# A list-scheduled Mamba layer and local transformer: a seventh tile for the broadcasts of B and C, paid with one tile for values and one for the shared sums, and a new order of all engines' work

## The chip, the core and the metric

The kernel runs on one core of a Trainium2 chip. The metric is the device time of one execution in microseconds (us); of several runs the median counts. A profiled execution gives a span, which is the time from the first to the last instruction, and its own device time.

The core's engines run side by side, each through its own list of instructions in order: PE (matrix products and transposes; results go to PSUM), DVE (vector work), ACT (activations and copies), POOL (elementwise work in SBUF), and SP, which here only issues DMAs. An instruction that waits for another engine or for a DMA holds everything behind it on its own engine.

## What is computed

The input x has 4096 rows of 256 numbers. Its layer-normed form xn goes into two branches, whose results are added to x:

```
x  = L0_attn_x
xn = _layernorm(x)
x  = x + mamba(xn) + ffn(xn)

# mamba, D_INNER 512, D_STATE 16
xz = xn @ in_proj_w.T;  x_inner, z = split(xz)
x_conv = silu(conv4(x_inner) + conv_b)
dt_lr, B, C = split(x_conv @ x_proj_w.T)          # 16 + 16 + 16 columns
dt = softplus(dt_lr @ dt_proj_w.T + dt_proj_b);   A = -exp(A_log)
h[t] = exp(dt[t] * A) * h[t-1] + (dt[t] * x_conv[t]) * B[t]
y[t] = sum over the 16 states of h[t] * C[t];     y += x_conv * D_param
out  = (y * silu(z)) @ out_proj_w.T

# ffn: two layers over the sequence of 4096 rows
q, k, v = shift(x) @ wqkv;  l2norm, scales, rotary;  8 heads, windows of 128 that see the one before
x = x + softmax(q k^T, masked) v @ wo
x = x + (a * gelu(g)) @ w2 + b2,   a, g = split(layernorm(shift(x)) @ w1 + b1)
```


## The kernel before, in words

**Work.** The transformer goes through 32 steps: layer 0 and then layer 1, each in 16 steps of 256 rows (two windows of 128). The Mamba branch goes through 8 blocks of 512 rows, each with 4 chunks of 128 channels, each chunk with 8 groups of two states: 256 groups in all. Block b and chunk c are tied to transformer step 4b + c, so one chunk of recurrences lies beside one transformer step.

**One group of the recurrence** (`recur`). Two DMAs bring rows of B and of C from memory, broadcast to all 128 partitions, into two tiles of the buffer `bc` (512 KB each). POOL multiplies the B tile by dt * x_conv in place (L793). For each of the two states ACT makes the decay (L802), DVE runs the recurrence over 512 steps (L807), ACT keeps the last state (L813), and DVE multiplies by the C tile (L817), writing over the B tile. In odd groups POOL adds the two states (L825); then PE sums the result into PSUM by transposes (L829). So the C tile is free after the second L817 and the B tile only after L829.

**Other parts that the change touches.** `normalize` loads rows of x into an `io` tile, and PE transposes them (L597). `project` makes q, k, v (L918), with L929 to L985 for norms and rotation and L945/L950 for the turned q and k; `attend` makes scores (L1017), mask and maximum (L1032), softmax (L1042), transposes (L1055), the copy to SBUF (L1059) and the product with v (L1071). `project_out` is L1112. `mlp` has means (L1141, after sums on POOL in L1149 and L1157), the up products (L1176), gelu (L1213), gains (L1221 on POOL), and the down products (L1247 in layer 0, L1266 in layer 1). `finish` (L546) adds a result to the shared sum of the two branches, which lies in an `io` tile, and stores it; `base_of` loads it again for the branch that comes second. `close` turns y back (L846 to L859), and `out_proj` is L879.

**The order.** Nothing is ordered by hand. Every operation is entered with an engine, a cost, a key (its step, less its own lead `soon`), and the tiles that it reads and writes. `Plan.order` is a list scheduler: it goes through time with these costs, gives each engine the open operation with the lowest key, and gives out the tiles of each buffer as they come free. Each engine's list is then issued as it came out, and on the chip the engines meet only at semaphores. On PE it takes into account that two kinds of product (`part="rows"`: L1017 and L734; `part="columns"`: L1071 and L702) use part of the array and that a change of kind costs. A DMA is counted as a fixed time plus its KB over a rate, and transfers on the way follow each other:

```
    TRANSFER, RATE = 2.2, 300.0
    ...
                w.end = moved = max(start + self.TRANSFER, moved) + w.late / self.RATE
```

Of the kernel before, what the change touches and what calls it, by code (L numbers as in the profile page):

```python
# [136 lines left out]
class Plan:  # L137
# [5 lines left out]
    TRANSFER, RATE = 2.2, 300.0  # L143
# [175 lines left out]
def mamba_and_local_transformer(  # L319
# [35 lines left out]
    rows_b = buffer("io", 3, [P, NW, D], any_first=True)  # L355
# [7 lines left out]
    values_b = buffer("v", 4, [P, INNER])  # L363
# [17 lines left out]
    spreads = buffer("bc", 6, [P, NG, TB])  # L381
# [73 lines left out]
    def load_small():  # L455
        dma(96, lambda: xpw.ap, lambda: xp_wT.rearrange("(c p) n -> p c n", p=P), writes=[xpw], soon=-0.25)
        for at_row in (0, DH):
            dma(32, lambda at_row=at_row: dtw.ap[at_row : at_row + DTR], lambda: dt_wT, writes=[(dtw, at_row)], soon=-1.44)
        dma(128, lambda: b2row.ap, lambda: b2_d[DEPTH - 1 : DEPTH, :].partition_broadcast(P), writes=[b2row], soon=-1.5)

    def load_qkv(l):
        for s in range(3):
            cut = slice(s * INNER, (s + 1) * INNER)
            dma(
                512, lambda cut=cut: wqkv.ap[:, :, cut],
                lambda cut=cut: wqkv_d[l][:, cut].rearrange("(k p) n -> p k n", p=P), writes=[(wqkv, s)], soon=0.31,
            )

    def load_rest(l):
        dma(512, lambda: wo.ap, lambda: wo_d[l].rearrange("(h p) n -> p h n", p=P), writes=[wo], soon=-0.19)  # L470
        for half in range(2):
            for m, n in ((0, WHOLE), (NM - 1, LAST)):
                to, of = w1_at(half, m), half * HID + m * MC
                dma(
                    n, lambda to=to, n=n: w1.ap[:, :, to : to + n],
                    lambda of=of, n=n: w1_d[l][:, of : of + n].rearrange("(k p) n -> p k n", p=P),
                    writes=[(w1, (half, m))], soon=-1.25,
                )
# [3 lines left out]
            lambda: w2_d[l][0:whole, :].rearrange("(m p) n -> p m n", p=MC), writes=[(w2, 0)], soon=0.22,  # L482
        )
        dma(42, lambda: w2.ap[0 : HID - whole, NM - 1, :], lambda: w2_d[l][whole:HID, :], writes=[(w2, 1)], soon=0.89)
# [28 lines left out]
        add("PE", 8.3, shift, [w1], [pb], soon=0.18)  # L513
        add("DVE", 0.4, bias, [pb], [b1, b1x], soon=0.05)
        add("DVE", 4.6, scale, [], [w1], port=True, soon=-0.44)
# [14 lines left out]
    def base_of(s):  # L530

        base = plan.value(rows_b)
        if s in sums:
            dma(256, lambda: base.ap, lambda: sums[s].ap, [sums[s]], [base], soon=-0.44)
            return base
        dma(256, lambda: base.ap, lambda: rows(x, s), writes=[base], soon=-1.19)
# [3 lines left out]
            ), [b2row], [base], soon=-0.45,  # L540
# [3 lines left out]
    def finish(s, po, base):  # L544

        add("DVE", 0.6, lambda: nc.vector.tensor_tensor(base.ap, halves(po), base.ap, ALU.add), [po], [base], soon=-0.18)  # L546
        if s in sums:
            dma(256, lambda: rows(out, s), lambda: base.ap, [base], soon=-1.5)
            return
        sums[s] = plan.fixed(dram.tile([P, NW, D], F32, tag=f"sum{s}", name=f"sum{s}"))  # L550
        dma(256, lambda: sums[s].ap, lambda: base.ap, [base], [sums[s]], soon=-1.32)
# [4 lines left out]
    def shift_column(l, s):  # L556
        now = xts[l, s]
        if s == 0:
            add("POOL", 0.14, lambda: nc.gpsimd.memset(now.ap[:, 1, 0:1], 0.0), [], [(now, 0)], soon=-0.18)
        else:  # L560
# [3 lines left out]
                [(old, 1)], [(now, 0)], soon=1.39,  # L564
            )

    def normalize(s):
# [5 lines left out]
        dma(256, lambda: xb.ap, lambda: rows(x, s), writes=[xb], soon=0.3)  # L573
# [27 lines left out]
        add("DVE", 1.1, stats, [xb], [mv], soon=1.36)  # L601
        add("ACT", 0.5, root, [mv], [rstd], soon=0.67)
        add("DVE", 0.6, centre, [mv, rstd], [xb], port=True, soon=-0.21)
        now = xts[0, s] = plan.value(tokens)
        add("PE", 0.44, turn, [xb], [pt], holds=[now], soon=1.2)
        add("ACT", 0.48, lambda: nc.scalar.copy(now.ap[:, :, 1:], halves(pt)), [pt], [(now, 1)], soon=0.88)
        shift_column(0, s)
        dma(256, lambda: xn_d[s].ap, lambda: now.ap[:, :, 1:], [(now, 1)], [xn_d[s]], soon=-0.42)
# [3 lines left out]
    def reload(s):  # L612
        now = xts[1, s] = plan.value(tokens)
        dma(256, lambda: now.ap[:, :, 1:], lambda: x1_d[s].ap, [x1_d[s]], [(now, 1)], soon=-0.52)
# [6 lines left out]
    def in_half(i):  # L621
# [3 lines left out]
            lambda: in_wT[:, i * DI : (i + 1) * DI].rearrange("(k p) n -> p k n", p=P), writes=[w], soon=-1.03,  # L625
# [3 lines left out]
    def in_proj(b, w, c, to):  # L629
# [9 lines left out]
        add("PE", 1.72, emit, [w, xms[b]], [pm], holds=[to], soon=-0.69)  # L639
        return pm  # L640

    def front_load(b):
        xm = xms[b] = plan.value(xms_b)
        for i in range(PB):
            s = b * PB + i
            dma(
                256, lambda i=i: xm.ap[:, :, i * TS : (i + 1) * TS], lambda s=s: xn_d[s].ap, [xn_d[s]], [(xm, i)], soon=-0.5
# [5 lines left out]
    def front_conv(b, c, w):  # L653
        xin, xc, tail = plan.value(rows_m), xcs[b], tails[b]
        edge = slice(c * (TAPS - 1), (c + 1) * (TAPS - 1))
        if b == 0:
            add("POOL", 0.14, lambda: nc.gpsimd.memset(xin.ap[:, 0 : TAPS - 1], 0.0), [], [(xin, 0)], soon=1.23)
        else:
# [3 lines left out]
                [(old, c)], [(xin, 0)], soon=1.08,  # L662
            )
        pm = in_proj(b, w, c, xin)
        add("ACT", 0.48, lambda: nc.scalar.copy(xin.ap[:, TAPS - 1 :], pm.ap), [pm], [(xin, 1)], soon=0.78)
        if b < NB - 1:
            add(
                "POOL", 0.14, lambda: nc.gpsimd.tensor_copy(tail.ap[:, edge], xin.ap[:, TB:]), [(xin, 1)], [(tail, c)], soon=0.17
# [5 lines left out]
            ), [], [pm], soon=-0.98,  # L674
# [8 lines left out]
        for j in range(TAPS - 1):  # L683
            add("DVE", 0.7, lambda j=j: tap(j), [xin, pm], [(xc, c) if j == TAPS - 2 else pm], soon=0.85)

    def silu(v):
# [4 lines left out]
        add("ACT", 4.52, emit, [], [v], soon=1.04)  # L691

    def front_dbl(b):
# [13 lines left out]
        add("PE", 1.75, emit, [xc, xpw], [px], holds=[xd, part], soon=-0.4, part="columns")  # L707
        add("ACT", 0.48, lambda: nc.scalar.copy(part.ap[0:n, 0:TB], px.ap[DH : DH + n]), [px], [part], alone=[px], soon=1.49)
# [5 lines left out]
        add("ACT", 0.48, lambda: nc.scalar.copy(xd.ap[DH : DH + DTR], xd.ap[0:DTR]), [(xd, 0)], [(xd, 1)], soon=-1.31)  # L714
        xds[b] = xd
        bc = bcs[b] = plan.fixed(dram.tile([2 * NS, TB], F32, tag=f"bc{b}", name=f"bc{b}"))
        dma(64, lambda: bc.ap, lambda: xd.ap[DTR:n, :], [(xd, 0)], [bc], soon=-0.54)

    def gate_conv(b, c, w):
# [4 lines left out]
        add("ACT", 0.48, lambda: nc.scalar.copy(sz.ap[:, c, :], pz.ap), [pz], [(sz, c)], soon=-1.26)  # L724

    def times(b, c):
# [12 lines left out]
        add("PE", 1.15, emit, [xd, dtw], banks2, holds=dts2, soon=0.95, part="rows")  # L739
        for i in range(2):  # L740
# [3 lines left out]
                ), [banks2[i]], [dts2[i]], soon=0.12,  # L744
# [3 lines left out]
    def prepare(b, c):  # L748

        if c % 2 == 0:  # L750
# [7 lines left out]
        add("ACT", 0.6, lambda: nc.scalar.activation(e.ap[:, n], dt.ap, AF.Abs), [dt], [e], soon=0.03)  # L758
        add("ACT", 0.6, lambda: nc.scalar.activation(dt.ap, dt.ap, AF.Relu), [], [dt], soon=-1.13)
        add("ACT", 0.54, lambda: nc.scalar.activation(e.ap[:, n], e.ap[:, n], AF.Exp, scale=-1.0), [], [e], soon=1.45)  # L760
        add(
            "DVE", 0.36, lambda: nc.vector.tensor_scalar(r.ap[:, n], e.ap[:, n], 1.0, -1.0, ALU.add, ALU.add),
            [e], [r], port=True, soon=1.5,
        )
        add("POOL", 1.22, lambda: nc.gpsimd.tensor_tensor(r.ap[:, n], e.ap[:, n], r.ap[:, n], ALU.subtract), [e], [r], soon=-0.4)
        add("ACT", 0.6, lambda: nc.scalar.activation(e.ap[:, n], e.ap[:, n], AF.Ln, bias=one_t), [], [e], soon=-0.27)
        add("POOL", 1.22, lambda: nc.gpsimd.tensor_tensor(dt.ap, dt.ap, r.ap[:, n], ALU.add), [r], [dt], soon=-1.2)
        add("POOL", 1.22, lambda: nc.gpsimd.tensor_tensor(dt.ap, dt.ap, e.ap[:, n], ALU.add), [e], [dt], soon=0.09)
# [653 lines left out]
```

## Time and profile before

| what | value |
|---|---|
| median of 3 runs | 1901.68 us (1895.44 to 1901.69) |
| the profiled execution's own time | 1896.31 us |
| its span | 1894.5 us |
| PE busy | 1853.1 us, 98% of the span |
| DVE, ACT, POOL busy | 1672.3 us (88%), 1588.8 us (84%), 1509.2 us (80%) |
| DMA | 334.69 MB, mean 177 GB/s |
| mean granted clock of PE | 0.993 |

How to read it: a row of the groups gives line, engine, operation, the tile written and the tiles read, shapes and count, then the busy time and the mean of one in ns, and last how long the engine stood idle before these instructions and who ended that. A row of the waits gives the sum, the number and the longest of such idle times. "SPq" is SP's queue of DMAs to issue: a wait there is the time in which the next DMA in order could not be issued. The float32 products of the program appear twice in the profile's counts.

### The profile page before, as it was taken

Reading aid. Unit: us, or ns where it says so; the run is one execution under the profiler, and the core shown is the slowest. Engines: PE = TensorE matmul, PEld = TensorE weight load, DVE = VectorE, ACT = ScalarE, POOL = GpSimd, SP = SyncE. Lnnn points to the kernel's source line nnn. Section 1 sums busy time; section 2 is a strip of 40 time slices with the busy share of each in tenths; the row PEclk is TensorE's granted clock in tenths of the full one; section 3 lists DMA queues with packets and bytes.
Section 4 is the critical chain, followed back from the end, with each engine's and each line's share of the span. In section 5 each row is a group of like instructions: output and inputs, shape, how many; then the busy total and the mean of one; then the engine's idle time right before and its main releaser. Section 6 shows DMA issues by size and latency. Waiting matters only on the chain.

```text
span 1894.5 us, 35774 instructions
## 1 busy us (share of the span) xinstructions
PE 1853.1 (98%) x12432; PEld 1419.8 (75%) x12432; DVE 1672.3 (88%) x3030; ACT 1588.8 (84%) x3794; POOL 1509.2 (80%) x1274
## 2 busy tenths in 40 slices
PE   7999999999999999999999999999999999999996
PEld 4767677777777777778678777777778787787885
DVE  6698999999998999799999888988989989889895
ACT  5789998889988889888896988988889878888783
POOL 4588888778888778878898786997878978788785
PEclk9899999999999999999999999999999999999999
DMA  5455455455555545456555654566454564445564
GB/s 188 134 177 172 158 175 188 169 179 179 166 178 180 186 152 192 157 186 206 177 199 188 208 166 142 169 204 215 154 160 162 192 221 162 159 161 173 170 215 147
DMA packets 133956, 334.69 MB, mean 177 GB/s; under 512 B 13468, under 2 KB 57200, under 8 KB 133776
## 3 DMA queue, kind: packets, MB, share of 16 engines
q1 hardware_dynamic: 133488, 332.21, 52.5%
q8 instruction: 98, 1.61, 0.3%
q14 instruction: 82, 0.67, 0.1%
q10 hardware_dynamic: 288, 0.20, 0.1%
HBM read 315.06 MB, written 17.30 MB: 175 GB/s over the span
## 4 chain that ended last, share of the span: by engine, by line
PE 42%; DVE 3%; ACT 2%; POOL 2%; DMA 1%; issue 1%; POOLq 0%; SPq 0%; DVEq 0%
PE mm L918 8%; PE mm L1176 8%; PE y L829 4%; PE mm L1266 3%; PE mm L1017 3%; PE mm L1071 3%; PE mm L1112 3%; PE mm L1055 2%; PE mm L635 2%; PE mm L879 2%; DVE da L807 1%; PE mm L950 1%; DMA bc<-bc 1%; POOL bc L793 1%; PE mm L1141 1%
## 5 line engine op out<-in xcount | busy, mean ns | idle before, releaser
L793 POOL TENSOR_TENSOR bc<-dtx,bc 128x1024 f32<-128x1024 f32 x256 | 607.0, 2372 | 130.5 <-DMA bc<-bc 96.8
L807 DVE TENSOR_TENSOR_SCAN da<-da,state,bc 128x512 f32<-128x512 f32 x448 | 563.2, 1278 | 53.1 <-POOL bc L793 22.2
L802 ACT ACTIVATE da<-dt,negA 128x512 f32<-128x512 f32 x512 | 349.6, 698 | 57.6 <-DVE bc L817 56.4
L918 PE MATMUL mm<-wqkv,xt 128*128 128x512 f32 x768 | 351.3, 597 | 2.8 <-DVE top L1032 2.6
L817 DVE TENSOR_TENSOR bc<-da,bc 128x512 f32<-128x512 f32 x512 | 337.2, 678 | 7.5 <-ACT state L813 5.1
L1176 PE MATMUL mm<-hn,w 128*128 128x256 f32 (+1 forms) x1408 | 330.9, 381 | 0.8 <-DVE top L1032 0.4
L1176 PEld LDWEIGHTS mm<-hn,w 128*128 128x128 f32 (+1 forms) x1408 | 255.1, 188 | 41.1 <-DVE top L1032 3.4
L1042 ACT ACTIVATE pr<-pr,top 128x256 f32<-128x256 f32 (+1 forms) x512 | 253.4, 500 | 10.1 <-DVE top L1032 9.6
L918 PEld LDWEIGHTS mm<-wqkv,xt 128*128 128x128 f32 x768 | 140.6, 191 | 141.6 <-issue 123.3
L1032 DVE CUSTOM_DVE_ANT_0 pr<-mm,maskf,nrm 128x256 f32<-128x256 f32 (+1 forms) x512 | 212.2, 472 | 17.5 <-PE mm L1017 13.4
L829 PE MATMUL y<-ident,bc 128*128 128x128 f32 x1536 | 217.9, 276 | 6.2 <-ACT m2k L846 2.6
L829 PEld LDWEIGHTS y<-ident,bc 128*128 128x128 f32 x1536 | 177.1, 141 | 54.5 <-issue 31.6
L985 POOL TENSOR_TENSOR turn<-turn,trig 128x512 f32<-128x512 f32 x128 | 161.5, 1283 | 57.5 <-DVE turn L978 57.5
L825 POOL TENSOR_TENSOR bc<-bc 128x512 f32<-128x512 f32 x128 | 164.3, 1283 | 39.2 <-DVE bc L817 38.9
L945 POOL TENSOR_TENSOR turn<-turn,turn 128x512 f32<-128x512 f32 x128 | 164.5, 1285 | 36.7 <-DVE turn L963 36.1
L1221 POOL TENSOR_TENSOR mlp<-mlp,ga 128x512 f32<-128x512 f32 (+2 forms) x128 | 127.3, 1006 | 18.4 <-ACT ga L1233 9.1
L1017 PEld LDWEIGHTS mm<-kT,qT 64*128 64x128 f32 x2016 | 118.9, 187 | 28.2 <-issue 11.2
L813 ACT COPY state<-da 128x1 f32<-128x1 f32 x448 | 72.7, 166 | 79.1 <-DVE da L807 72.4
L1059 ACT COPY prT<-mm 128x512 f32<-128x512 f32 (+1 forms) x256 | 134.8, 591 | 4.3 <-PE mm L1055 3.6
L1071 PE MATMUL mm<-prT,v 128*64 128x128 f32 x2016 | 136.6, 280 | 1.3 <-ACT prT L1059 1.3
L1071 PEld LDWEIGHTS mm<-prT,v 128*64 128x64 f32 x2016 | 112.8, 136 | 33.0 <-issue 10.1
L1017 PE MATMUL mm<-kT,qT 64*128 64x128 f32 x2016 | 134.1, 280 | 0.0
(132 smaller groups left out, 3563.6 us busy)
## 6 DMA issues: line engine op xcount, KB each, us to landing
bc<-bc SPq DMA_DIRECT2D x512, 512.0 KB, 4.4
io<-in_x SPq DMA_DIRECT2D x32, 256.0 KB, 5.1
mw<-in_in_wT SPq DMA_DIRECT2D x16, 512.0 KB, 3.7
rot<-in_rot SPq DMA_DIRECT2D x32, 128.0 KB, 2.6
xn<-xt SPq DMA_DIRECT2D x16, 256.0 KB, 3.9
xm<-xn SPq DMA_DIRECT2D x16, 256.0 KB, 5.0
x<-mid SPq DMA_DIRECT2D x16, 256.0 KB, 4.6
mw<-in_out_wT SPq DMA_DIRECT2D x8, 512.0 KB, 5.3
```

Source lines behind the costliest of these rows:

```text
L793: "POOL", 2.35, lambda: nc.gpsimd.tensor_tensor(u.ap, dtx.ap.unsqueeze(1).to_broadcast([P, NG, TB]), u.ap, ALU.mult), [dtx], [u], soon=-0.45,
L802: "ACT", 0.63, lambda h=h, n=n: nc.scalar.activation(h.ap, dt.ap, AF.Exp, scale=negA[:, c * NS + n : c * NS + n + 1]), [dt], [h], soon=-0.12,
L807: "DVE", 1.18, lambda h=h, n=n, i=i: nc.vector.tensor_tensor_scan(h.ap, h.ap, u.ap[:, i, :], state.ap[:, c, n : n + 1] if b else 0.0, ALU. ...
L817: "DVE", 0.61, lambda h=h, i=i: nc.vector.tensor_tensor(u.ap[:, i, :], h.ap, spread[1].ap[:, i, :], ALU.mult), [h, spread[1]], [(u, i)], a ...
L829: nc.tensor.matmul(y.ap[:, t, :], lhsT=u.ap[:, i, t * P : (t + 1) * P], rhs=ident, is_transpose=True, start=g == 0 and i == 0 and t == 0, ...
L918: nc.tensor.matmul(pm.ap, lhsT=hT[k], rhs=wqkv.ap[:, k, q * INNER : (q + 1) * INNER], start=k == 0, stop=k == KC - 1,)
L945: add("POOL", 1.22, lambda: nc.gpsimd.tensor_tensor(parts[0].ap, parts[0].ap, parts[1].ap, ALU.add), [parts[1]], [parts[0]], soon=0.21)
L1017: nc.tensor.matmul(halves(scs[j])[:, i, a * WIN : (a + 1) * WIN], lhsT=qT.ap[half, 2 * g + i, :], rhs=kk.ap[half, 2 * g + i, :], start=n == 0,
L1032: nc.vector.tensor_tensor_reduce(out=prs[j].ap[:, i, keys], in0=halves(scs[j])[:, i, keys], in1=mask[:, keys], scale=nrm.ap[:, h : h + 1], ...
L1042: nc.scalar.activation(prs[j].ap[:, i, keys], prs[j].ap[:, i, keys], AF.Exp, bias=top.ap[:, h : h + 1], scale=-1.0, accum_out=den.ap[:, h ...
L1071: nc.tensor.matmul(hpair(po.ap)[j * DH : (j + 1) * DH, hp, :], lhsT=vv.ap[:, h * DH : (h + 1) * DH], rhs=prT.ap[:, j, a, :], start=a == first,
L1176: nc.tensor.matmul(halves(pm)[0:r, i, :], lhsT=w1.ap[:, k, c0 : c0 + r], rhs=hn.ap[:, k, :], start=k == 0, stop=k == KC - 1,)
```

## The change

Three buffers change their number of tiles: `bc` from 6 to 7, `v` (the values, of which a window needs its own and the one before) from 4 to 3, `io` (rows of x and the shared sums) from 3 to 2. The scheduler counts a DMA as 2.3 us plus KB at 270 per us in place of 2.2 and 300, so a 512 KB load as 4.2 us in place of 3.9, and the product with v as 1.0 in place of 0.93. All the leads `soon` have new values. The instructions that are issued are the same, in a new order; which tile an operation gets changes too.

```diff
-    TRANSFER, RATE = 2.2, 300.0
+    TRANSFER, RATE = 2.3, 270.0
...
-    rows_b = buffer("io", 3, [P, NW, D], any_first=True)
+    rows_b = buffer("io", 2, [P, NW, D], any_first=True)
...
-    values_b = buffer("v", 4, [P, INNER])
+    values_b = buffer("v", 3, [P, INNER])
...
-    spreads = buffer("bc", 6, [P, NG, TB])
+    spreads = buffer("bc", 7, [P, NG, TB])
...
-        dma(96, lambda: xpw.ap, lambda: xp_wT.rearrange("(c p) n -> p c n", p=P), writes=[xpw], soon=-0.25)
+        dma(96, lambda: xpw.ap, lambda: xp_wT.rearrange("(c p) n -> p c n", p=P), writes=[xpw], soon=-0.84)
         for at_row in (0, DH):
-            dma(32, lambda at_row=at_row: dtw.ap[at_row : at_row + DTR], lambda: dt_wT, writes=[(dtw, at_row)], soon=-1.44)
-        dma(128, lambda: b2row.ap, lambda: b2_d[DEPTH - 1 : DEPTH, :].partition_broadcast(P), writes=[b2row], soon=-1.5)
+            dma(32, lambda at_row=at_row: dtw.ap[at_row : at_row + DTR], lambda: dt_wT, writes=[(dtw, at_row)], soon=-0.13)
+        dma(128, lambda: b2row.ap, lambda: b2_d[DEPTH - 1 : DEPTH, :].partition_broadcast(P), writes=[b2row], soon=-0.82)
...
-                lambda cut=cut: wqkv_d[l][:, cut].rearrange("(k p) n -> p k n", p=P), writes=[(wqkv, s)], soon=0.31,
+                lambda cut=cut: wqkv_d[l][:, cut].rearrange("(k p) n -> p k n", p=P), writes=[(wqkv, s)], soon=-0.17,
...
         u = spread[0]
         add(
             "POOL", 2.35, lambda: nc.gpsimd.tensor_tensor(
                 u.ap, dtx.ap.unsqueeze(1).to_broadcast([P, NG, TB]), u.ap, ALU.mult
-            ), [dtx], [u], soon=-0.45,
+            ), [dtx], [u], soon=-0.28,
...
-                ), [h, spread[1]], [(u, i)], alone=[h], soon=-0.33,
+                ), [h, spread[1]], [(u, i)], alone=[h], soon=-0.32,
...
             add(
-                "PE", 0.93, mix, prTs + [vv for _, _, vv in pieces], [(po, g)], holds=[] if g else [OT], soon=1.5,
+                "PE", 1.0, mix, prTs + [vv for _, _, vv in pieces], [(po, g)], holds=[] if g else [OT], soon=1.25,
                 part="columns",
             )
```

The lead of the bc loads themselves (`soon=-0.76` in `recur`) is unchanged; the other leads change in the same way as those shown.

## The prediction

> **What bounds the kernel now.** I read the busy line of the page first, then the table of stretches, then the waits engine by engine, then the chain, and last the timeline of the end.
>
> ```profile
> PE 1853.1 (98%) x12432; PEld 1419.8 (75%) x12432; DVE 1672.3 (88%) x3030; ACT 1588.8 (84%) x3794; POOL 1509.2 (80%) x1274
> ```
>
> PE is busy for all but 41.4 us of the span. The stretches say where these lie (columns: us, busy time and count of PE, PEld, DVE, ACT, POOL, PE's granted clock, DMA share, GB/s):
>
> ```profile
> 0.00:100.00 100.00, 87.26 (x497) 59.71 (x498) 66.45 (x159) 69.53 (x165) 51.22 (x75) 0.95 0.52 166
> 100.00:950.00 850.00, 840.93 (x5679) 639.37 (x5680) 779.23 (x1426) 738.42 (x1796) 694.50 (x586) 1.00 0.53 176
> 950.00:1800.00 850.00, 845.74 (x5750) 653.83 (x5749) 754.04 (x1348) 721.36 (x1712) 696.33 (x571) 1.00 0.53 178
> 1800.00:1894.50 94.50, 79.21 (x511) 66.91 (x509) 72.61 (x100) 59.52 (x124) 67.13 (x45) 0.96 0.52 181
> ```
>
> So 12.7 us are lost in the first 100 us, 13.3 us in the 1700 us between, and 15.3 us in the last 94.5. No new order can win more than these 41.4 us, less what start and end can't avoid, plus what PE loses inside its busy time. The waits of POOL and of SP's queue (us in total, times, longest):
>
> ```profile
> POOL bc L793 <- DMA bc<-bc: 96.8, 65, 4.6
> ...
> SPq L453 <- DVE bc L817: 712.9, 200, 14.7
> SPq L453 <- PE y L829: 469.8, 198, 7.7
> ```
>
> For 1182.6 us of the span the next DMA in SP's order stands there because a `bc` tile is not yet free: the six tiles set when the loads of B and C start, and 65 times POOL then waits for the landing. But POOL has 20% to spare; what matters is how much of this PE feels:
>
> ```profile
> PE mm L597 <- DVE io L589: 8.6, 1, 8.6
> PE mm L1266 <- POOL mlp L1221: 7.7, 3, 4.2
> ...
> PE y L829 <- POOL bc L825: 2.4, 4, 1.0
> PE mm L1141 <- POOL sq L1157: 2.1, 2, 1.1
> PE mm L950 <- POOL turn L945: 2.1, 2, 1.5
> ```
>
> Behind the start (8.6) and the end (L1266), only 6.6 us of PE's waits in the middle go to POOL. The chain of work that ended last is PE from step to step through nearly all of 950 to 1640; a part of it also gives the price of a change of PE's kind of product:
>
> ```profile
> 1778.41 1.95 PE mm L1071 x32
> 1780.36 0.59 PE y L829 x4
> 1780.95 0.44 PE mm L1097 x4
> ```
>
> Four transposes take 0.44 us, and 0.59 right behind the product with v, which uses half of the columns: 0.15 us per change. At the end the recurrence is the bound, as POOL's timeline shows:
>
> ```profile
> 1860.25 2.36 POOL L793 TENSOR_TENSOR bc<-dtx,bc 128x1024 f32<-128x1024 f32 x1 [0.16 <-DMA bc<-bc]
> 1864.20 2.34 POOL L793 TENSOR_TENSOR bc<-dtx,bc 128x1024 f32<-128x1024 f32 x1 [1.60 <-DMA bc<-bc]
> ```
>
> **The change part by part.** The sum is made against the profiled execution: span 1894.5, own time 1896.31. The median of the runs, 1901.68, lies 5.4 us above that; I add the differences to the median. Both kernels issue the same instructions, so each term is about order. I counted along the order in which each kernel issues on each engine, which follows from the code, and priced the counts with the rows above.
>
> *Seventh bc tile.* In SP's order a tile is loaded again for a group on average 3.0 groups later before, 3.5 after. A group lasts 7.0 us (the first L793 is at 73.2, the 256th at 1869.1), so loads can start 3.5 us earlier. POOL's 65 waits average 1.5 us and the longest is 4.6, so I expect most of the 96.8 us to go. POOL's next limit is then DVE: L825 waits 38.9 us for L817, L985 57.5 us for L978; these stay. PE gains at most its 6.6 us on POOL, at least nothing, since the waits for L1157 and L945 hang on DVE and ACT too. I take half: -3.3.
>
> *The transfers in the scheduler.* A bc load took 4.4 us (median from issue to landing). The old count for it was 3.9, the new one is 4.2: still short, but nearer. This has no instruction of its own; its worth is that fewer steps stand too tight. For each of 1,752 steps on PE I compared the PE work that stands between it and the step its operand comes from with the durations of the links between: 114 steps have under 0.5 us to spare before, 85 after. The 5.7 us of PE's gaps in the middle that go to ACT and DVE (13.3 less 6.6, less 1.0 for L879's weights) scaled by 85/114: -1.4; ends -5.7 and, since a new order deals new gaps, +5.7.
>
> The page "DMA: Bandwidth & Descriptors" of the Trainium skill (Anatomy of one DMA) speaks against this part: it gives a fixed 2.0 us plus bytes over 436 GB/s, fitted for DMAs of the GpSimd path, which would be 3.2 us for 512 KB as an estimate. By that both counts would already be too long, an earlier load would gain nothing, and the sum below would be -6.1 instead of -11. The 4.4 us and the 65 waits in the trace are of this kernel, so I go by them.
>
> *Changes of PE's kind.* Along PE's order the kind changes 376 times before, 361 after. 15 x 0.15 = -2.3; ends -1.5 and -3.0 (0.10 and 0.20 each; behind the scores L1017 the chain has 1.92 us for eight L1176 that otherwise take 1.73).
>
> *The end.* When the last L1112 has been issued, DVE has 42.9 us of work left in the old order and 39.5 in the new (18 and 17 scans at 1.28, the rest by their rows). From there to the last scan DVE is the engine that sets the end, so -3.4 (ends -3.4 and 0, if DVE then waits for something else). The wait of 1.60 us for a load at 1864.20 goes with the earlier loads: -1.6 (ends -1.6 and 0). Behind the last L829, close, L879 and the store stand as before.
>
> *The start.* In SP's queue the three wqkv loads stood behind two io loads and xpw; now dtw (twice, 32 KB) and b2row (128 KB) go ahead of them too, and tile 1 of x lands without them beside it. The added 192 KB take 0.6 us at the 311 GB/s of the stretch from 10 to 20 us, and three more issues at 0.45 us 1.3. In the old trace x was turned at 10.3, yet ACT got the first L918 only at 13.48 and the next at 15.20, 1.72 later: the first was late by about 1.2, so it has no slack towards wqkv. Against this DVE waited 1.59 us for tile 1's rows, which would shrink. Ends -1.6 and +3; I take +1.0, between issue and bytes. PE's work ahead of the first L829 is the same (67.8 and 67.9 us).
>
> *One tile less for v and io.* Before, four v tiles were in use at once during 155 us of PE's work only; with three, every product into a v tile still stands behind the last read of it in PE's order, and the ACT copy that really waits comes later. Cost 0; the cover is that distance, at least 0.6 us, and without it the copy L991 (0.59 us) would hold ACT. For io, a load that stands within three places of a store from the same tile in SP's queue holds the bc loads behind it for up to a store's 3.9 us: 20 of 33 before, 21 of 38 after. Cost 0; if the cover of the longer bc lead were gone, one more such wait is 3.9 us on POOL.
>
> Sum: -3.3 - 1.4 - 2.3 - 5.0 + 1.0 = -11.0. Span 1883.5, median 1890.7. The ends give -6.6 - 5.7 - 3.0 - 5.0 - 1.6 = -22 (1880) and 0 + 5.7 - 1.5 + 0 + 3.0 = +7 (1909).
>
> **The rivals.**
>
> *PE is full and its gaps are only dealt anew.* For it: PE lost just 4.3 us between 950 and 1800, so POOL's 96.8 us are nearly all hidden. Against it: the end is not hidden. Changes of kind -2.3 and the start +1 to +3 remain: 1900 to 1902.
>
> *The loads start no earlier.* SP is in order, and L546 held it for 74.7 us in 22 waits; with two io tiles this could take the half group back. Then POOL keeps its 96.8, and -3.3 and -1.6 drop out: -6.1, so 1895.6.
>
> *Slower: POOL's in-order queue in front of PE.* The seventh tile lets L793 (2.37 us) be drawn forward on POOL, ahead of the sums L945 and L1157 that PE waits for. In the first recurrences of the new order four L793 stand nearly in a row. The trace has such gaps: 1.50 us at L950 and 1.11 at L1141 around 940. With one of 1.3 us in each of 32 transformer steps it would be 42 us in place of 6.6; with the other terms (-7.7) +27.7, so 1929. It decides from 24 us, 18 gaps, more than every second step. Against it: POOL has 385 us idle, and the spare counts above improve.
>
> **How the numbers follow.** 0.5% of the median is 9.5 us. Likeliest case 0.50; gaps dealt anew 0.15; loads no earlier 0.08; slower 0.27. The prediction is the likeliest's 1890.7, its own range 1880 to 1903. The range of all reaches down to 1879 and, as the slower case has more than 2 in 10, up to such a gap in 22 of 32 steps, +14.3 us: 1916. Below 1892.2 lies a little over half of the likeliest case and a part of the others' tails; as its terms hang together (all gain if the loads come earlier) I put 0.50 there, within 0.5% 0.23; above 1911.2 0.27.
>
> **What would show it.** The wait of L793 for bc falls below 40 us and SP's two rows below 1100; 2 to 3 us less between PE's groups; PE's idle time in the last 94 us under 11, in the first 100 us 13 to 15, in between under 11. PE's waits on L945, L1157 and L825 over 20 us would mean the third rival; L793's wait still near 97 the second. I am wrong above all if the middle loses more than 25 us.

## The result, and the profile after

| | before | after |
|---|---|---|
| median of 6 runs each, us | 1900.6 (1895.44 to 1904.51) | 1889.75 (1888.21 to 1891.13) |
| ratio, 95% interval | | 0.9947 (0.9929 to 0.9965) |
| profiled execution, own time, us | 1896.31 | 1890.55 |
| its span, us | 1894.5 | 1888.8 |

The change makes the kernel 0.5% faster: 10.9 us by the medians. The two profiled executions differ by only 5.7 us of span. Half of the gain is therefore not in this pair of profiles, and an experiment below follows a part of it: the old kernel's executions scatter over 9 us, the new one's over 3, and the profiled execution of before was one of its shortest.

The busy line of the page after:

```profile
PE 1850.9 (98%) x12432; PEld 1422.4 (75%) x12432; DVE 1667.1 (88%) x3030; ACT 1588.7 (84%) x3794; POOL 1508.6 (80%) x1274
```

PE's busy time falls by 2.2 us, its idle time from 41.4 to 37.9. The same stretches as before (us, busy time and count of PE, PEld, DVE, ACT, POOL, PE's granted clock, DMA share, GB/s):

```profile
0.00:100.00 100.00, 88.59 (x493) 59.11 (x494) 66.84 (x161) 69.94 (x165) 52.65 (x77) 0.95 0.48 156
100.00:950.00 850.00, 838.70 (x5650) 639.54 (x5649) 776.15 (x1422) 736.62 (x1791) 693.08 (x583) 1.00 0.54 177
950.00:1800.00 850.00, 847.42 (x5788) 657.84 (x5787) 760.20 (x1362) 727.29 (x1729) 701.14 (x573) 1.00 0.54 181
1800.00:1888.80 88.80, 76.20 (x506) 65.92 (x504) 63.89 (x89) 54.89 (x113) 61.74 (x43) 0.95 0.52 172
```

PE now loses 11.4 us in the first 100 us, 13.9 in the middle and 12.6 at the end; before it was 12.7, 13.3 and 15.3. The middle, 1700 us long, gives nothing in this pair. The waits (sum, times, longest):

```profile
POOL bc L825 <- DVE bc L817: 65.2, 37, 6.5
POOL turn L985 <- DVE turn L978: 63.0, 33, 3.2
...
POOL bc L793 <- DMA bc<-bc: 44.7, 33, 3.6
...
PE mm L950 <- DVE hn L1167: 2.6, 1, 2.6
...
PE mm L950 <- POOL turn L945: 1.4, 4, 0.5
...
PE y L829 <- POOL bc L825: 0.7, 2, 0.5
```

The loads of B and C do come earlier. POOL's wait for them halves (96.8 to 44.7), and its next limit grows, the waits for DVE at L825 (38.9 to 65.2). PE's waits for POOL in the middle nearly vanish, from 6.6 to 1.6 us, but its waits there for ACT and DVE grow from 5.9 to 11.8. One of them, 2.62 us at 142.90, is longer than any of the old ones on POOL (1.5). The sums of SP's queue:

```profile
SPq L453 <- DVE bc L817: 645.5, 197, 10.3
SPq L453 <- PE y L829: 499.4, 202, 11.4
SPq L453 <- DVE io L546: 94.1, 26, 15.6
```

SP stands 1144.9 us for `bc` tiles in place of 1182.7, and 94.1 us at L546 in place of 74.7.

### The profile page after: what moved, and what is told of

Same layout as the page of the kernel before. It is cut to its first block, busy times and chain, and to the rows that moved or that the text cites. A ratio compares the mean times of both kernels' runs of the same rounds, so it can differ in the third digit from the quotient of the medians.

```text
span 1888.8 us, 35786 instructions
## 1 busy us (share of the span) xinstructions
PE 1850.9 (98%) x12432; PEld 1422.4 (75%) x12432; DVE 1667.1 (88%) x3030; ACT 1588.7 (84%) x3794; POOL 1508.6 (80%) x1274
## 5 line engine op out<-in xcount | busy, mean ns | idle before, releaser
L793 POOL TENSOR_TENSOR bc<-dtx,bc 128x1024 f32<-128x1024 f32 x256 | 605.7, 2368 | 80.7 <-DMA bc<-bc 44.7
L802 ACT ACTIVATE da<-dt,negA 128x512 f32<-128x512 f32 x512 | 349.2, 698 | 49.7 <-DVE bc L817 47.9
L918 PE MATMUL mm<-wqkv,xt 128*128 128x512 f32 x768 | 353.5, 598 | 1.4 <-DVE top L1032 0.8
L817 DVE TENSOR_TENSOR bc<-da,bc 128x512 f32<-128x512 f32 x512 | 338.3, 679 | 5.8 <-ACT state L813 3.7
L918 PEld LDWEIGHTS mm<-wqkv,xt 128*128 128x128 f32 x768 | 139.7, 191 | 137.0 <-issue 121.2
L825 POOL TENSOR_TENSOR bc<-bc 128x512 f32<-128x512 f32 x128 | 165.3, 1291 | 71.5 <-DVE bc L817 65.2
L829 PE MATMUL y<-ident,bc 128*128 128x128 f32 x1536 | 219.6, 277 | 2.2 <-ACT m2k L846 1.5
L829 PEld LDWEIGHTS y<-ident,bc 128*128 128x128 f32 x1536 | 177.1, 141 | 58.6 <-issue 40.0
L945 POOL TENSOR_TENSOR turn<-turn,turn 128x512 f32<-128x512 f32 x128 | 164.2, 1283 | 32.4 <-DVE turn L965 31.4
L1059 ACT COPY prT<-mm 128x512 f32<-128x512 f32 (+1 forms) x256 | 133.9, 595 | 3.4 <-PE mm L1055 3.1
L1071 PE MATMUL mm<-prT,v 128*64 128x128 f32 x2016 | 134.5, 281 | 0.0
L1071 PEld LDWEIGHTS mm<-prT,v 128*64 128x64 f32 x2016 | 113.8, 137 | 25.1 <-issue 8.8
L1055 PE MATMUL mm<-ident,pr 128*128 128x128 f32 x1008 | 130.5, 276 | 2.0 <-ACT qT L956 0.9
```

Source lines behind the costliest of these rows:

```text
L793: "POOL", 2.35, lambda: nc.gpsimd.tensor_tensor(u.ap, dtx.ap.unsqueeze(1).to_broadcast([P, NG, TB]), u.ap, ALU.mult), [dtx], [u], soon=-0.28,
L802: "ACT", 0.63, lambda h=h, n=n: nc.scalar.activation(h.ap, dt.ap, AF.Exp, scale=negA[:, c * NS + n : c * NS + n + 1]), [dt], [h], soon=0.0,
L817: "DVE", 0.61, lambda h=h, i=i: nc.vector.tensor_tensor(u.ap[:, i, :], h.ap, spread[1].ap[:, i, :], ALU.mult), [h, spread[1]], [(u, i)], a ...
L825: add("POOL", 1.22, lambda: nc.gpsimd.tensor_tensor(u.ap[:, 0, :], u.ap[:, 0, :], u.ap[:, 1, :], ALU.add), [], [u], soon=-1.1)
L829: nc.tensor.matmul(y.ap[:, t, :], lhsT=u.ap[:, i, t * P : (t + 1) * P], rhs=ident, is_transpose=True, start=g == 0 and i == 0 and t == 0, ...
L918: nc.tensor.matmul(pm.ap, lhsT=hT[k], rhs=wqkv.ap[:, k, q * INNER : (q + 1) * INNER], start=k == 0, stop=k == KC - 1,)
```

## The experiments

Twelve kernels were run. In one group (`i`, `f`, `g`, `h`, `p`, `o`) the kernel is changed directly, or in `o` not at all. In the other (`j`, `d`, `m`, `e`, `n`, `k`) the planner's order is kept as it was made, and a buffer then gets another number of tiles than was planned for. An added pass goes through the planned order, gives out the tiles again, and lets a step that would need a tile not yet free follow right behind the step that frees it:

```diff
-        for w in self.order():
+        for w in self.settle(self.order()):
```

The pass lengthens the file by 68 lines, so in this group L793 reads L861, L825 L893, L829 L897, L945 L1013, L817 L885, L1059 L1127 and L1071 L1139. T1 is the theory that the tile brings the gain by earlier loads, T2 that the new order brings it.

### A second profile of the kernel before

The kernel is unchanged.

> The kernel before, unchanged, for a second profile. If its waits are the same in each execution, the span is within 1 us of 1894.5, and L793's wait within 3 us of 96.8. If before's executions differ because its bc loads just miss POOL, the span lies up to 10 us higher, L793's wait is longer by several us, and PE's waits for POOL exceed 6.6 us in the middle; the gain of after against the usual execution is then larger than the 5.7 us between the two first profiles, by this. The ratio to before must hold 1.

Measured: median 1899.84 us of 12 runs (1897.56 to 1906.53), ratio to before 1.0004 (0.9992 to 1.0015). The profiled execution took 1906.53 us, span 1904.7, so it is one of the longest. Its waits:

```profile
POOL bc L793 <- DMA bc<-bc: 119.3, 76, 4.7
...
DVE bc L817 <- DMA bc<-bc: 1.3, 2, 0.8
```

POOL waits 22.5 us more for the loads than in the first profile (96.8), as the second half of the expectation says. But PE's waits for POOL in the middle are 6.8 us against 6.6, so that part of it missed: the loss takes another way, and it can be followed. Around 1810 both executions issue the same work. In the second one DVE's L817 waits 0.84 us for a C tile (DVE, then POOL and PE, each with its start, its duration and its wait in brackets):

```profile
1812.00 0.67 DVE L978 TENSOR_TENSOR turn<-mm,nrm 128x512 f32<-128x512 f32 x1
1813.51 0.69 DVE L817 TENSOR_TENSOR bc<-da,bc 128x512 f32<-128x512 f32 x1 [0.84 <-DMA bc<-bc]
1814.12 1.28 DVE L807 TENSOR_TENSOR_SCAN da<-da,state,bc 128x512 f32<-128x512 f32 x1
1815.31 2.56 DVE L762 TENSOR_SCALAR m2k<-m2k 128x512 f32<-128x512 f32 x1
1817.80 0.68 DVE L546 TENSOR_TENSOR io<-mm,io 128x512 f32<-128x512 f32 x1
```

```profile
1815.22 2.37 POOL L793 TENSOR_TENSOR bc<-dtx,bc 128x1024 f32<-128x1024 f32 x1
```

```profile
1818.53 0.66 PE L1055 MATMUL mm<-ident,pr 128*128 128x128 f32 x4 [2.06 <-DVE io L546]
```

L762 now starts 0.09 us behind a long L793 of POOL and takes 2.56 us; in the first profile it took 1.17 at this place, and PE's L1055 did not wait at all. DVE's L546 is late by the 0.84 and by these 1.39 us, and PE stands for 2.06. From 1819.43 to 1822.84, right behind this wait, PE's granted clock is at half, which makes the products there take about another 1.6 us. From this L1055 to the last L1112 the second execution falls back by 3.9 us (3.8 behind the first one at the first of them, 7.7 at the other), and behind it by another 2.5; there L793 waits 2.38 us for a load where it waited 1.60. The 3.8 us before that come from many small pieces and from a place around 955, where PE ran at a lower granted clock (told in the last section). In all the second execution has 2.8 us more idle time on PE and 7.4 us more busy time.

So the old order's loads arrive just in time or just too late, from execution to execution, and at one place this is seen to cost some 4 us. No more of the scatter than that is traced to a load: the 3.2 us at 955 come from the clock, behind a wait that is the same in both executions. Against the mean span of the two profiles of before (1899.6) after is 10.8 us shorter, close to the difference of the medians; that all of the difference to the first pair comes from late loads is not shown.

### Two variants that leave the order of after nearly alone

The wqkv loads go in front, right behind the first two io loads:

```diff
-        for w in self.order():
+        done = self.order()
+        sp = [w for w in done if w.engine == "SP"]
+        first = sp[6:9]
+        done = [w for w in done if w not in first]
+        at = done.index(sp[1]) + 1
+        for w in done[:at] + first + done[at:]:
```

> The changed kernel with the three wqkv loads put back to their old place in SP's queue, right behind the first two io loads and ahead of dtw, b2row and xpw; all else as in the changed kernel. My step of the start (wqkv comes later: +1.0 us): the first products L918 end about 1 us earlier and so does the whole, -0.5 to -1.5 us. Rival: tile 1's rows then land later again (first L597 back from 7.5 to about 8.6 us) and nothing is won: 0 to +0.5.

And in the order of after three io tiles, paid with one kT tile; no step moves:

```diff
+    rows_b = buffer("io", 2, [P, NW, D], any_first=True, real=3)
+    keys_b = buffer("kT", 3, [P, HP, P], real=2)
```

> The changed kernel with three io tiles instead of two in an otherwise unchanged order (room from one tile less for kT). My step (one io tile less costs 0): the time stays within 1 us. Rival (with two io tiles the loads behind a store hold SP's queue: its wait for L546 is 94.1 us in the changed kernel): SP's wait for L546 falls by half and the time by 2 to 4 us.

Measured: 1891.52 us (1890.34 to 1892.81), ratio 0.9949 (0.9933 to 0.9965), for the loads in front; 1889.16 (1888.72 to 1893.53), ratio 0.9941 (0.9924 to 0.9958), for three io tiles. Neither is to be told from after, so in both it is the expectation of no effect that came: the later wqkv loads cost nothing that shows, and an io tile more, with a kT tile less as its price, changes nothing either. SP's wait at L546 (L614 there) stays at 94.6 us with three io tiles. As both issue nearly what after issues, they also serve as repeats of its profile. Sums of PE's idle time and waits, in us, from the stretches and the waits of the five profiles:

| | before | before again | after | wqkv in front | three io |
|---|---|---|---|---|---|
| span | 1894.5 | 1904.7 | 1888.8 | 1889.0 | 1887.1 |
| PE idle, first 100 us | 12.7 | 12.0 | 11.4 | 13.1 | 11.2 |
| PE idle, 100 to 1800 | 13.3 | 14.2 | 13.9 | 11.0 | 10.7 |
| in it, waits for POOL | 6.6 | 6.8 | 1.6 | 1.0 | 0.8 |
| in it, waits for ACT, DVE, DMA | 6.9 | 6.9 | 11.8 | 9.5 | 9.1 |
| PE idle from 1800 on | 15.3 | 17.9 | 12.6 | 13.5 | 12.6 |
| end of the last L1112 to the span's end | 57.7 | 60.2 | 54.4 | 55.5 | 54.9 |
| PE busy | 1853.1 | 1860.5 | 1850.9 | 1851.4 | 1852.6 |

In all three profiles of the new order PE waits 5 to 6 us less for POOL, 2 to 5 us more for the others, and the end is 2 to 6 us shorter. From the mean of the two profiles of before to the mean of the three others the span falls by 11.3 us: PE's busy time by 5.2, and its idle time by 3.7 from 1800 on, by 1.9 in the middle and by 0.5 in the first 100 us. So almost half of the gain is time in which PE counts as busy. The mean granted clock is 0.993 and 0.991 before and 0.992 in the other three, so the clock doesn't explain it; 1.3 us of it are fewer changes of kind (told below), and the rest was not traced.

### The seventh tile in the old order

First paid with one kT tile and one `turn` tile; seven steps move:

```diff
+    turns = buffer("turn", 4, [P, HEADS, 2, DH // 2], real=3)
+    keys_b = buffer("kT", 3, [P, HP, P], real=2)
+    spreads = buffer("bc", 6, [P, NG, TB], real=7)
```

> The order of before, kept instruction by instruction (7 of 8,760 steps move a little), with seven bc tiles; room for the seventh comes from one tile less for kT (which never holds more than two values in that order) and one less for turn. Theory 1 (the tile: loads that start earlier take away POOL's waits, and PE gains from that): POOL's wait of L793 for bc falls from 96.8 to under 50 us and the time by 4 to 8 us. Theory 2 (the order: changes of kind, the shorter end, more to spare): the wait falls too, but the time by 0 to 3 us only, since the end's 42.9 us of DVE work and the 376 changes of kind stay.

Measured: 1910.79 us (1908.06 to 1914.21), ratio 1.0050 (1.0033 to 1.0067). Its waits:

```profile
POOL turn L1053 <- DVE turn L1046: 81.4, 39, 8.3
...
POOL bc L861 <- DMA bc<-bc: 42.9, 32, 3.2
...
PE mm L1018 <- POOL turn L1013: 9.9, 5, 4.5
```

POOL's wait for the loads falls as in after. But PE now waits 9.9 us for the sums L1013 (2.1 before), so the missing `turn` tile spoils the trial. It was repeated with an io tile as the price, one of the two that the change itself pays; 52 steps move, 32 of them io loads:

```diff
+    rows_b = buffer("io", 3, [P, NW, D], any_first=True, real=2)
+    keys_b = buffer("kT", 3, [P, HP, P], real=2)
+    spreads = buffer("bc", 6, [P, NG, TB], real=7)
```

> The order of before kept as it was planned, with seven bc tiles in place of six, paid with one io tile (3 to 2) and one kT tile (3 to 2) instead of with a turn tile as in d_old_order_7; 52 steps shift to keep the order free of deadlock, 32 of them io loads in SP's order. T1 (the tile as such brings the gain): POOL's wait at L793 for bc falls from 96.8 to about 45 us, as in d_old_order_7, PE's waits for POOL from 6.6 us in the middle to about 2, and the time to 1894 to 1897, at least 4 us below before. T2 (the order brings it): L793's wait falls in the same way, but the order was laid out for six tiles, so PE's gaps stay, and the time is 1898 to 1903. If two io tiles do harm, it is slower than 1905 with SP's wait at L546 over 90 us.

Measured: 1988.21 us (1982.35 to 1994.53), ratio 1.0464 (1.0446 to 1.0483).

```profile
POOL io L606 <- DMA io<-in_x: 60.5, 13, 6.8
...
POOL bc L861 <- DMA bc<-bc: 43.2, 27, 5.6
...
PE y L897 <- POOL bc L893: 25.9, 10, 4.1
...
PE mm L1018 <- POOL turn L1013: 13.9, 8, 3.9
```

The last case of the expectation came, far beyond its bound, with SP's wait at L546 (L614 here) at 115.9 us. With two io tiles the rows of x are loaded late, POOL stands 60.5 us at L606 (L538) for them, and everything behind it in its in-order queue is late; PE's waits for POOL come to 52.0 us in place of 15.2 over the span. With an io and a kT tile less the order made for three io tiles loses 88 us, where the order made for two loses nothing. What the seventh tile is worth by itself in the old order thus stays unmeasured, as both payments outweigh it, and T1 is neither shown nor refuted. What both trials do show is that a wait at L793 that is halved doesn't make up for a missing `turn` or io tile.

### The new order without the seventh tile

```diff
+    spreads = buffer("bc", 7, [P, NG, TB], real=6)
```

> The order of the changed kernel with six bc tiles (441 loads are issued later, 26 multiplies L793 move behind a neighbour; PE, DVE and ACT keep their order). Theory 1 (the tile): L793's wait for bc rises from 44.7 to 90 us or more and 4 to 8 us of the gain are lost against the changed kernel. Theory 2 (the order): the wait rises, and the time by 0 to 3 us.

Measured: 2113.91 us (2111.16 to 2117.02), ratio 1.1116 (1.1093 to 1.1138); by the two ratios 11.8% slower than after.

```profile
POOL bc L861 <- DMA bc<-bc: 328.6, 115, 9.0
...
PE y L897 <- POOL bc L893: 63.5, 33, 6.6
...
PE mm L1018 <- POOL turn L1013: 48.1, 30, 4.5
```

Here the mechanism of the third rival is at work: L861 (L793) waits for loads in POOL's in-order queue, and PE's waits for POOL come to 153.3 us. So the new order brings nothing without the tile, which speaks against T2 in its plain form, and both expectations missed the size by far: 224 us are lost against after, in place of 4 to 8 or 0 to 3. The order was laid out around loads that start a tile earlier, and 441 loads and 26 multiplications by POOL move without it.

### An eighth tile, and its control

In the order of after, an eighth tile paid with a kT tile and a prT tile, and then the same payment without the eighth tile (the diff without its last line); 30 steps move in each:

```diff
+    keys_b = buffer("kT", 3, [P, HP, P], real=2)
+    probs_T = buffer("prT", 4, [P, 2, 2, P], real=3)
+    spreads = buffer("bc", 7, [P, NG, TB], real=8)
```

> The changed kernel's order with eight bc tiles (room from one tile less for kT and one less for prT; 30 of 8,760 steps move a little). Theory 1 (tile): L793's wait for bc falls from 44.7 to under 20 us and the time by another 2 us or more. Theory 2 (order): the wait falls and the time stays within 1 us, or rises where prT is missing.

> The order of after with its seven bc tiles, and prT 3 and kT 2, so the same sacrifice as in k_new_order_8 without the eighth bc tile; 30 steps shift. If the missing prT tile made k_new_order_8 slower (1909.63), this one is as slow, 1907 to 1913, with ACT's copy of prT waiting about 30 us for PE's product with v. If the eighth bc tile itself does harm, this one is near after, 1889 to 1893. If it is slower than k_new_order_8 by 4 us or more, an eighth tile has a worth of its own even in the order made for seven.

Measured: 1909.63 us (1906.95 to 1914.93), ratio 1.0040 (1.0017 to 1.0064), with the eighth tile; 1909.99 (1904.86 to 1912.03), ratio 1.0045 (1.0032 to 1.0058), without it. The waits with eight tiles:

```profile
ACT prT L1127 <- PE mm L1139: 30.5, 40, 2.2
...
POOL bc L861 <- DMA bc<-bc: 24.1, 14, 3.8
```

and with seven:

```profile
POOL bc L861 <- DMA bc<-bc: 46.1, 37, 4.3
...
ACT prT L1127 <- PE mm L1139: 30.1, 41, 1.2
```

The 20 us over after are thus the price of the payment, and since a kT tile less cost nothing in the run with three io tiles, of the prT tile: ACT's copy into it now waits 30 us for PE's product with v. By which way this reaches PE was not followed. The eighth tile itself halves L793's wait once more, by 22 us (to 24.1, not under 20 as T1 had it), and moves the time by nothing that can be measured; the two intervals leave room for some 5 us either way, so T1's further 2 us are not excluded.

### Parts of the change, planned anew

Here the planner was left to make a new order for a part of the change. The tiles alone, in the kernel before:

```diff
-    rows_b = buffer("io", 3, [P, NW, D], any_first=True)
+    rows_b = buffer("io", 2, [P, NW, D], any_first=True)
-    values_b = buffer("v", 4, [P, INNER])
+    values_b = buffer("v", 3, [P, INNER])
-    spreads = buffer("bc", 6, [P, NG, TB])
+    spreads = buffer("bc", 7, [P, NG, TB])
```

> Before with the new numbers of tiles alone (bc 7, v 3, io 2), scheduled anew with the old leads and the old costs of transfers. If the tile by itself brings the gain (theory 1): -4 to -8 us against before. If the gain lies in an order whose leads fit its tiles (theory 2): between -3 and +10 us, as the leads were not made for these tiles.

The counted costs and the leads without the tiles, in the kernel after:

```diff
-    rows_b = buffer("io", 2, [P, NW, D], any_first=True)
+    rows_b = buffer("io", 3, [P, NW, D], any_first=True)
-    values_b = buffer("v", 3, [P, INNER])
+    values_b = buffer("v", 4, [P, INNER])
-    spreads = buffer("bc", 7, [P, NG, TB])
+    spreads = buffer("bc", 6, [P, NG, TB])
```

> The changed kernel with the old numbers of tiles (bc 6, v 4, io 3), scheduled anew with the new leads and costs. Theory 1 (tile): near before, 1898 to 1903. Theory 2 (order): if the new leads are good of themselves, 1889 to 1894; if they only fit seven tiles, over 1900.

The tiles and the leads without the counted costs:

```diff
-    TRANSFER, RATE = 2.3, 270.0
+    TRANSFER, RATE = 2.2, 300.0
...
-                "PE", 1.0, mix, prTs + [vv for _, _, vv in pieces], [(po, g)], holds=[] if g else [OT], soon=1.25,
+                "PE", 0.93, mix, prTs + [vv for _, _, vv in pieces], [(po, g)], holds=[] if g else [OT], soon=1.25,
```

> The changed kernel with the old costs in the scheduler (2.2 us and 300 KB per us for transfers, 0.93 for the product with v), scheduled anew with the new leads and tiles. If the longer transfers in the scheduler matter: L793's wait for bc rises over 60 us and the time by 2 to 6 us. If they don't: within 2 us of the changed kernel, or a change that is not tied to this wait.

And a control in which one lead of after differs by 0.06 and nothing else does:

```diff
-                add("ACT", 0.98, soft, [(top, (g, j))], [prs[j], (den, (g, j))], soon=-1.08)
+                add("ACT", 0.98, soft, [(top, (g, j))], [prs[j], (den, (g, j))], soon=-1.14)
```

> The kernel after with the lead of the softmax L1042 changed from -1.08 to -1.14 and nothing else; the planner then lays out nearly all of the order anew. If the leads of after are one point of a rough surface, in which any new order costs a few per cent, this is 1910 to 1960 in spite of the same tiles and costs. If the tiles and the counted transfers make the time by themselves, and leads matter little, it is within 0.5% of after, 1880 to 1899.

| kernel | us | ratio to before, 95% | L793's wait, us |
|---|---|---|---|
| tiles only | 1945.74 | 1.0242 (1.0218 to 1.0266) | 108.3 |
| costs and leads only | 1947.6 | 1.0250 (1.0221 to 1.0279) | 112.8 |
| tiles and leads only | 2010.06 | 1.0576 (1.0538 to 1.0614) | 157.6 |
| after with one lead changed | 1947.01 | 1.0239 (1.0223 to 1.0254) | 93.9 |

The stretches of the last one:

```profile
100.00:950.00 850.00, 820.13 (x5520) 622.48 (x5519) 766.17 (x1381) 712.32 (x1735) 672.58 (x567) 1.00 0.53 173
950.00:1800.00 850.00, 839.82 (x5637) 643.56 (x5635) 746.77 (x1327) 726.97 (x1719) 690.88 (x567) 0.99 0.54 177
```

With all tiles and all counted costs of after, one lead changed by 0.06 loses 30 us of PE in the first stretch and 10 in the second, and L793 waits 93.9 us again with seven tiles. The control costs 57 us against after, as much as leaving out a whole part does. It lies within its first expectation, 1910 to 1960; the kernel with the tiles only (45 us over before, where -8 to +10 was expected) and the one without the counted costs (120 us over after, where 2 to 6 was expected) missed theirs by far. So the first two kernels of the table say nothing about the worth of the part that they leave out; they show what an order costs that was not searched for. Only the third, 63 us above the control, may show that the leads lean on the counted costs, and with one control this is not settled.

## Why the prediction was right, and where it was not

The forecast was 1890.7 us and the median is 1889.75. The likeliest case came about, in the sense that the loads come earlier, POOL waits less, PE waits less for POOL and the end gets shorter. Term by term, against the first profile of before, for which the sum was made:

| step of the prediction | predicted, us | measured, us |
|---|---|---|
| seventh tile: PE's waits for POOL in the middle | -3.3 | -5.0 |
| longer transfers: PE's waits for ACT and DVE in the middle | -1.4 | +5.9 |
| the wait for L879's weights in the middle | 0 | -1.0 |
| changes of PE's kind | -2.3 | -1.3, from their number and mean price |
| the end, from the last L1112 | -5.0 | -3.3 |
| the start | +1.0 | -1.3 (PE idle in the first 100 us) |
| span | -11.0 | -5.7 |

The rows don't add up to the last one, since the end is measured over all engines; PE's idle time in the start, the middle and the end and its busy time do (-1.3, +0.6, -2.7, -2.2). Of the sizes that the prediction named as signs none was met in this pair: L793's wait and SP's two rows fell by less (below), and PE's idle time is 12.6 us at the end in place of under 11, 11.4 in the first 100 us in place of 13 to 15, and 13.9 between in place of under 11.

*Seventh tile.* The mechanism was right and its size was between the bounds. L793's wait fell to 44.7 us, not under 40, and SP's two rows to 1144.9, not under 1100: I took half a group of earlier loads as if nothing else held SP's order, but its waits at L546 grew by 19.4 us.

*Longer transfers.* This is the step that failed. Fewer steps with under 0.5 us to spare (85 for 114) did not mean fewer gaps: PE's waits for ACT and DVE doubled, and 2.6 of the 5.9 us are a single one, PE's L950 for DVE's L1167 at 142.90. The number of these waits doesn't follow the count either: 15 in before, 18, 15 and 15 in the three profiles of the new order. What grew is their length, from 0.39 us on average to 0.66, 0.63 and 0.61, and the one of 2.6 us stands in all three. The count says how many steps are tight and not how late a late one is. The upper end of +5.7 was written for just that, "a new order deals new gaps". In the other two profiles of the new order these waits are 3.6 and 3.2 us above before, so a part of the size in one profile is chance. Why this order makes its gaps longer was not found.

*Changes of kind.* The mechanism holds. The traces show the 376 and 361 changes too, and where the clock is full and PE doesn't wait, the step from one kind to the other takes 0.152 us more than the same product's usual step in both profiles of before, on average, and 0.155 in the three of the new order. That makes 57.3 us in all before and 56.0 after, so -1.3. That PE's busy time fell by 2.2 us in the first pair is no evidence: two executions of the unchanged kernel before differ by 7.4 in it.

*The end.* DVE's shorter work behind the last L1112 came, and the wait of 1.60 us at 1864.20 is gone with its gap of 3.86 us in DVE. In its place stands a gap that I had not looked for (DVE and ACT of after):

```profile
1862.38 2.47 DVE L807 TENSOR_TENSOR_SCAN da<-da,state,bc 128x512 f32<-128x512 f32 x2 [2.56 <-ACT da L802]
```

```profile
1857.20 1.28 ACT L1213 ACT_TABLE_LOAD   x1
1858.49 1.49 ACT L1213 ACTIVATE mlp<-mlp 128x1536 f32<-128x1536 f32 x1
1859.99 1.28 ACT L1214 ACT_TABLE_LOAD   x1
1861.29 0.47 ACT L1233 ACTIVATE ga<-mm,b 128x256 f32<-128x256 f32 x1
1861.66 1.29 ACT L802 ACTIVATE da<-dt,negA 128x512 f32<-128x512 f32 x2
```

The last gelu holds ACT from 1857.20 to 1861.27 with two table loads of 1.28 us around it, and the decays L802 that DVE needs stand behind it in ACT's order. I asked what ended DVE's wait for the load, but not what was late next.

*The start.* The term had the wrong sign, and its working misread a row: the first L918 of before was not late for its weights. It starts at 10.36 us, right behind the turned x, and PE's products then follow each other 1.02 to 0.85 us apart, until 12.6 us, and 0.43 us apart behind that; the trace's record of the full clock begins at 12.61. In after it begins at 13.62, the steps get short there, and the first 20 products L918 take 1.04 us longer. Tile 1's rows land sooner without the wqkv loads beside them (the first L597 is at 7.51 in place of 8.60), and the first products end at 20.26 in place of 20.31. Loads put in front again gain nothing, which the run with wqkv in front confirms.

*One tile less for v and io.* For io the cost of 0 is shown by the run with three tiles; for v it is not, as v was not tried by itself. The trial in the old order shows how much the cover matters there: 88 us without it.

*The median.* The sum of -11.0 was added to the median, and the median moved by 10.9; but the profiled pair moved by 5.7 only. The first profile of before was a short execution, so it lacked what its longer ones lose, in part to late loads. My sum was too large for the pair it was made for, and the steadier executions that it had no term for made up the rest. The forecast was right in its main mechanism, fewer waits of PE for POOL and a shorter end, and lucky in its size: that it lies within 1 us of the median is chance.

The rivals: PE's waits for L945, L1157 and L825 in the middle are under 3 us, so POOL's queue did not become the bound; the run with six tiles shows that it can (153.3 us of waits). "The loads start no earlier" is out by L793's 44.7 us. "The gaps are only dealt anew" describes the middle of the first pair well, and is out for the whole by the median, 1889.75 in place of 1900 to 1902, and by the shorter end.

## What to carry to other kernels

When the wait that a change removes stands close to the edge, profile the kernel before more than once: half of this gain didn't show against the first profile, a short execution. In a kernel whose order is searched, the worth of tiles, counted costs and leads can't be had by taking them out one by one, as this mostly measures an order that was not searched for; a control with one tiny lead changed says how much of a loss is only that. A wait on an engine that isn't the bound has to be followed to what waits behind it: L793's wait was halved four times here, and only once did the time fall, though the other three had given up a tile for it.

## What the runs showed of the hardware

**A gap of 1.5 us can cost PE its clock, or not.** In both profiles of before PE stands 1.50 us ahead of the same L950. The timeline of the first:

```profile
951.77 0.66 PE L950 MATMUL mm<-ident,turn 128*128 128x128 f32 x4 [1.50 <-POOL turn L945]
952.36 1.13 PE L734 MATMUL mm<-xd,dtw 16*128 16x512 f32 x4
953.42 1.16 PE L1017 MATMUL mm<-kT,qT 64*128 64x128 f32 x16
954.52 1.99 PE L918 MATMUL mm<-wqkv,xt 128*128 128x512 f32 x4
```

and of the second:

```profile
954.75 0.66 PE L950 MATMUL mm<-ident,turn 128*128 128x128 f32 x4 [1.50 <-POOL turn L945]
955.33 1.59 PE L734 MATMUL mm<-xd,dtw 16*128 16x512 f32 x4
956.86 2.08 PE L1017 MATMUL mm<-kT,qT 64*128 64x128 f32 x16
958.87 3.78 PE L918 MATMUL mm<-wqkv,xt 128*128 128x512 f32 x4
```

In the first the granted clock stays at 1.00; in the second it is 0.59 from 955 to 960 and 0.73 from 960 to 965, and the same three groups take 3.2 us longer. So the same gap costs 1.5 us in one execution and 4.7 in another. The Trainium skill ("TensorE: Matmul & The Clock Gate", Part 1) lets the clock fall after an idle window of about 3.4 us and calls the window free-running. The gap here is less than half as long, so by the measurement gaps well under 3.4 us are not safe. Why the two executions differ can be read from the trace's records of the granted clock. In each execution they change on a grid of 3.41 us only, which lies elsewhere each time. In the second, the period from 952.44 to 955.86 holds the whole gap (953.24 to 954.75), and from its end the clock is at half for two periods. In the first, the grid cuts the gap (950.28 to 951.77) at 951.27. The old order with seven tiles and a `turn` tile less has the same 1.50 us, whole in the period from 950.06 to 953.48, and the clock is at half from 953.48 to 960.30. In all fourteen profiles, behind the first 70 us, 81 periods at the full clock held 2.0 us of idle time on PE or more, and the next period was at half each time; of the 45 with 1.5 to 2.0 us this holds for 8. In the slower experiments the clock follows the gaps: mean 0.979 with 94 us of idle time on PE (the old order with two io tiles) and 0.965 with 200 us (the new order with six `bc` tiles), against 0.992 with 38 us in after. Their PE is busy for longer too, by 36 and 64 us over after.

**Some DVE instructions wait inside themselves for POOL.** L762 of DVE takes 0.41 us where POOL is between instructions, and up to 2.56 us where it starts during one. In after, 21 of its 32 take more than 0.45 us, and all of these end 0.28 to 0.29 us behind the end of a POOL instruction that ran beside them. L972 shows the same: 0.16 us at the median in after, and 3.51 at most, beside three POOL instructions in a row. The two rows at 1810.56 in the first profile of before, DVE's and POOL's:

```profile
1810.56 1.17 DVE L762 TENSOR_SCALAR m2k<-m2k 128x512 f32<-128x512 f32 x1
```

```profile
1808.93 2.52 POOL L985 TENSOR_TENSOR turn<-turn,trig 128x512 f32<-128x512 f32 x2 [0.75 <-DVE turn L978]
```

They end at 1811.73 and 1811.45. The page "SBUF — State Buffer" of the Trainium skill (SBUF: two separate sides) tells of a port pair that a POOL instruction and a DVE instruction in a two-port mode take from each other for their whole length. The trace agrees as far as DVE waits for POOL; it doesn't say whether L762 runs in such a mode. The wait shows up as a longer instruction and not as a wait in any row, and it makes a small lateness larger: with L793 (2.37 us) in front of it, the 0.84 us of a late load became 2.06 us on PE.
